# Twelve layers in one planned graph: the last block laid into the same plan and the same memory as the layers before it

## The chip, the cores and the metric

The kernel runs on one core of one Trainium2 chip. Its time is the device time of one execution in microseconds (us), taken as the median of several runs. Everything is float32, but for some masks in bfloat16.

## The reference

A decoder of four layers with three sublayers each, on `x` of 4 x 256 x 128 (batch, tokens, width), every sublayer added to its input:

```python
x = x + L0_attn(layernorm(x))
x = x + L0_xattn(layernorm(x), ctx_768, ...)
x = x + L0_ffn(layernorm(x), ...)          # grouped attention and experts
...
x = x + L2_attn(layernorm(x), ...)
x = x + L2_xattn(ctx_768, layernorm(x), mask, ...)
x = x + L2_ffn(layernorm(x), ...)          # 4-bit quantised, gated
x = x + L3_attn(layernorm(x), ...)
x = x + L3_xattn(layernorm(x), ctx_768, ...)   # 16 heads of 64
x = x + L3_ffn(layernorm(x), ...)          # six layers of local attention and a gated unit
```

The last sublayer, `L3_ffn`, is as long as a small network of its own:

```python
for i in range(6):
    x = attn_layer(shift_tokens(x), Wqkv[i], q_scale[i], k_scale[i], Wo[i]) + x
    x = ffn_layer(shift_tokens(x), ln_g[i], ln_b[i], W1[i], b1[i], W2[i], b2[i]) + x
```

`attn_layer` has 16 heads of 64; queries and keys are divided by their norm, scaled and turned by a rotary table, and every window of 32 queries sees its own and the previous 32 keys. `ffn_layer` is a layernorm, a product to 2 x 341, a gelu on one half, a product of the halves and a product back to 128.

## The kernel before

The kernel is a planner with two plans. Class `Flow` takes operations one by one (`op`): each has an engine, a weight (the time that the planner believes it takes), a unit of work, and the buffers that it reads, writes or holds. `order` then plays the graph through: at each step the operation that can start first is issued, and between several that can start the one with the earliest due time. A due time follows from the unit's place in the sequence of TensorE work (`bases`, stretched by a pace) and a number of its own for each kind of operation (the third entry in the tables `NET` and `LOCAL`). Each kind of buffer has a fixed number of slots; `vacant` tells when a slot is free. The instructions are written in that order, and on each engine they run in it.

Class `Net` plans the eleven sublayers up to `L3_xattn`: the stages are generators that yield after each batch, and the string `ORDER` says in which order their batches follow. Its last stages are `ffn2`, `attn3` and `X3`, the last for `L3_xattn`. Every kind of buffer is a set of tiles in pools that are closed when `Net` ends.

Class `LocalBlock` plans the last sublayer with another `Flow`, in pools of its own that take the memory that `Net` has given up:

```python
    with ExitStack() as early:
        d = Decoder(early, tc, a, const)
        d.prepare()
        with ExitStack() as own:
            Net(own, d).run()
    if "F3" in STEPS:
        LocalBlock(ctx, d).run()
```

`LocalBlock.run` first writes, outside of any plan, its constants (`prepare`: the rotary tables by SP, the window mask and memsets on POOL, L1780 to L1817) and its input (`start`: a layernorm of each batch, two transposes at L1824, copies on ACT at L1826 into `y`, which holds two batches with features on partitions). Then come six layers of four units, one for each batch (`unit`), and after every second batch a gated unit for both (`glu`). The weights of a layer are loaded by `load`, issued on ACT (L1840). A unit's steps bear these names in the plan: `project` (query and key products, L1775 through the helper `mm`), `square` (ACT, L1919), `cosine` and `turned` (DVE, L1921 and L1911), `rotary` (POOL, L1925), `norms`, `guess` and `newton` (DVE: inverse norms), `scale` (POOL, L1963), `turn` (transposes, L1973) and their copies (L1980), `scores`, `most`, `less`, `exp`, `sums` and `share` (POOL, L2007), `turn_p` (L2048) and its copies (L2053), `values`, `weigh`, `weigh_out` (L2071) and `out`. `finish` turns `y` back, adds it to `x` and stores, again outside of the plan.

In `Net` all products go through L371 and all transposes through L374; copies out of PSUM are at L379. L735 to L753, L646 to L653 and so on are the softmax steps of its attentions.

Of the kernel before, what the change touches and what calls it, by code (L numbers as in the profile page):

```python
# [66 lines left out]
class Decoder:  # L67
# [5 lines left out]
    def small(self, n, tag):  # L73
        return self.sm.tile([P, n], F32, tag=tag, name=tag, bufs=4)

# [7 lines left out]

    def rsqrt(self, out, in_, n, scale, eps, op=ALU.add):

        self.nc.vector.tensor_scalar(out, in_, scale, eps, ALU.mult, op)
        self.nc.gpsimd.tensor_tensor(out, out, self.neghalf[:, :n], ALU.pow)

    def layernorm(self, src, out, eps=1e-5):

        nc, n = self.nc, src.shape[1]
        st = self.small(6 * 4, "ln_st").rearrange("p (t s) -> p t s", s=6)
        mv = self.small(2 * 4, "ln_mv").rearrange("p (t s) -> p t s", s=2)
        rstd = self.small(4, "ln_rs")
        for t in range(n):
            nc.vector.bn_stats(st[:, t, :], src[:, t, :])
            nc.vector.bn_aggr(mv[:, t, :], st[:, t, :])
        self.rsqrt(rstd[:, :n], mv[:, :n, 1], n, 1.0, eps)
        for t in range(n):
            nc.vector.tensor_scalar(  # L100
                out[:, t, :], src[:, t, :], mv[:, t, 0:1], rstd[:, t : t + 1], ALU.subtract, ALU.mult
            )
# [63 lines left out]
class Flow:  # L166
# [11 lines left out]

    LAG = {"PE": 0.22, "ACT": 0.1, "DVE": 0.1, "POOL": 0.12, "SP": 2.5}
# [7 lines left out]
    def __init__(self, kinds, pace, patience, slots, lags, tables, tiles, free=(), dense=(), port=()):  # L187
        self.kinds, self.pace, self.slots, self.lags, self.tables = kinds, pace, slots, lags, tables
        self.patience, self.tiles, self.dense, self.port = patience, tiles, dense, port
        self.free, self.ops, self.counts = free, [], dict.fromkeys(slots, 0)  # L190

    def op(self, name, unit, fn, reads=(), writes=(), holds=()):
        eng, weight, late = self.kinds[name]
        op = {
            "name": name, "eng": eng, "w": weight, "late": late, "unit": unit, "fn": fn,
            "lag": self.lags.get(name, self.LAG[eng]), "table": self.tables.get(name),
# [21 lines left out]
    def bases(self):  # L218
        work = {}
        for op in self.ops:  # L220
            work[op["unit"]] = work.get(op["unit"], 0.0) + op["w"] * (op["eng"] == "PE")
        at, out = 0.0, {}
        for unit in sorted(work):
            at += work[unit] * self.pace
            out[unit] = at
        return out

    def order(self):
# [12 lines left out]
        made = dict.fromkeys(self.slots, 0)  # L241
# [21 lines left out]
        while len(done) < len(self.ops):  # L263
# [4 lines left out]
            for e, ops in waiting.items():  # L268
# [4 lines left out]
                if times:  # L273
                    first = min(t for t, *_ in times)
                    late = lambda o: o["due"] + (
                        (self.patience if o["tiles"][0] != shape else 0.0)
# [33 lines left out]
    def vacant(self, kind):  # L310

        out = []
        for slot, b in enumerate(self.held[kind]):
            if b is None:
                out.append((0.0, slot))
            elif all("end" in o for o in b.users):
                out.append((max(o["end"] + o["lag"] for o in b.users), slot))
        return sorted(out)

    def issue(self):  # L320
        for op in self.order():
# [3 lines left out]
            op["fn"]()  # L325


class Net:
# [12 lines left out]
        "top": (16, 6), "tr": (2, 6), "ss": (16, 2), "qs": (48, 4), "row": (128, 3),  # L341
    }
    SLOTS = {"bank": 8, "pad0": 2, "pad8": 2, "vb": 2, "vs": 2} | {k: n for k, (_, n) in TILES.items()}

    def __init__(self, ctx, d):
# [3 lines left out]
        tables = {k: "e" for k in NET if k.endswith("_exp")}  # L349
        self.flow = Flow(NET, NET_PACE, NET_PATIENCE, self.SLOTS, {"fetch": 6.0}, tables, NET_TILES, ("bank",))  # L350
# [6 lines left out]
    def buf(self, kind):  # L357
        if kind == "bank":
            return Buffer(kind, lambda i: self.pb.tile([P, 512], F32, tag=f"bank{i}", name=f"bank{i}", bufs=1))
        n, _ = self.TILES[kind]  # L360
        return Buffer(kind, lambda i: self.sb.tile([P, n], F32, tag=f"{kind}{i}", name=f"{kind}{i}", bufs=1))
# [641 lines left out]
    def prepare(self):  # L1003
        nc = self.nc
        make = lambda n, name: self.sb.tile([P, n], F32, tag=name, name=name, bufs=1)
        self.pads, self.vss, self.vbs = {}, [], []
        for hole in self.HOLE:
            self.pads[hole] = []
            for i in range(self.SLOTS[f"pad{hole}"]):
                m = make(256, f"pad{hole}_{i}")  # L1010
                nc.gpsimd.memset(m, 0.0)
                self.pads[hole].append(m)
        for i in range(2):

            v = make(1040, f"vs{i}")
# [3 lines left out]
        for i in range(2):  # L1019
            v = make(576, f"vb{i}")  # L1020
# [656 lines left out]
    def write(self):  # L1677
        stages = {name: getattr(self, f"stage_{name}")() for name in STEPS if name != "F3"}
        for name in ORDER.split():
            if name in stages:  # L1680
                next(stages[name])

# [42 lines left out]
class LocalBlock:  # L1725
# [15 lines left out]
        "qk": (1024, 5), "sq": (1024, 2), "tmp": (1024, 2), "ss": (64, 2), "rs": (64, 2),  # L1741
        "qT": ((8, P), 2), "mx": (16, 2), "p": (1024, 2), "rz": (16, 2), "vn": (1024, 3),
        "v": (1024, 2), "pT": ((8, P), 2), "oT": ((8, S), 1), "g_sq": (512, 1), "g_xc": (512, 1),
        "g_var": (4, 1), "g_rstd": (4, 1), "uT": ((3, 512), 1), "tab": ((2, 2, 2, 64), 2), "b1": (6, 2),
        "w4": (1024, 7), "w1": (2 * FF3, 2), "w2": ((3, D), 2),
    }
    SLOTS = {"bank": 8, "kT": 2} | {k: n for k, (_, n) in TILES.items()}

    def __init__(self, ctx, d):
        self.d, self.tc, self.nc, self.a = d, d.tc, d.nc, d.a  # L1750
        pool = lambda name, **kw: ctx.enter_context(self.tc.tile_pool(name=name, bufs=1, **kw))
        self.c, self.sb = pool("l_const"), pool("l_work")
        self.pb = pool("l_pb", space=PSUM)
        d.sm = self.sb
        tables = {"exp": "e", "gelu": "g"}
# [867 lines left out]
```

## Time and profile before

| | us |
|---|---|
| median of 3 runs | 2145.88 (2144.1 to 2146.22) |
| the profiled execution's own time | 2146.45 |
| span of the profiled execution | 2144.7 |
| TensorE busy in the span | 2040.7 (95%) |
| VectorE busy | 1635.6 (76%) |
| ScalarE busy | 1181.0 (55%) |
| GpSimd busy | 986.2 (46%) |

PE is TensorE, PEld its weight loads, DVE VectorE, ACT ScalarE, POOL GpSimd, SP the engine that issues most transfers. A row of the profile names line, engine, operation, the tiles written and read, and how often. "PEclk" is the clock that the throttle grants to TensorE, as a share of full speed; a busy TensorE at half clock does half the work. A float32 product appears as two records of TensorE. In a table of stretches each row is a part of the span with the busy time of each engine in it; in the chain of waits each piece is followed back to what released it.

### The profile page before, as it was taken

The numbers are of one execution on the slowest core, as the hardware profiler recorded it, in microseconds if no ns is written. First come the engines' busy times: TensorE is split into PE (matmuls) and PEld (weight loads), VectorE is DVE, ScalarE is ACT, GpSimd is POOL, SyncE is SP. The second block draws the span as 40 slices with busy tenths as digits, with TensorE's granted clock in tenths as the row PEclk, the third lists the DMA queues.
The fourth block names the chain that finished last, engine by engine and source line by source line (L and its number), as shares of the span: only waits on it lengthen the run. The fifth ranks groups of instructions, "written<-read, shape, count | busy, mean of one in ns | idle before, by whom it ended". The sixth has DMA issues, their size and how long they took to land.

```text
span 2144.7 us, 58806 instructions
## 1 busy us (share of the span) xinstructions
PE 2040.7 (95%) x24181; PEld 1347.1 (63%) x24181; DVE 1635.6 (76%) x4353; ACT 1181.0 (55%) x2668; POOL 986.2 (46%) x1152
## 2 busy tenths in 40 slices
PE   7999999999999998899999977999999999999997
PEld 4566585776665566566666644666666666666665
DVE  3766777788777758989986548978789787897882
ACT  1754736434536676566556534556555555565553
POOL 2333424331312234445333357756557565575660
PEclk6999999999999999899999988999999999999998
DMA  5000020002020000100000031112121121121101
GB/s 153 1 1 1 1 65 6 31 31 64 2 75 1 9 2 5 45 1 1 1 1 1 1 102 31 42 34 69 42 71 44 42 69 42 38 65 42 37 26 31
DMA packets 33419, 71.14 MB, mean 33 GB/s; under 512 B 5688, under 2 KB 17984, under 8 KB 33152
## 3 DMA queue, kind: packets, MB, share of 16 engines
q1 hardware_dynamic: 20320, 50.29, 8.1%
q10 hardware_dynamic: 12832, 17.09, 2.5%
q8 instruction: 191, 3.13, 0.6%
q14 instruction: 76, 0.62, 0.1%
HBM read 41.68 MB, written 0.52 MB: 20 GB/s over the span
## 4 chain that ended last, share of the span: by engine, by line
PE 70%; DVE 19%; POOL 5%; issue 3%; ACT 2%; DMA 1%; POOLq 0%; SPq 0%; DVEq 0%; ACTq 0%
PE bank L371 40%; PE bank L1775 18%; PE bank L374 8%; PE bank L1973 2%; DVE tmp L1911 2%; DVE ss L1926 2%; POOL qk L1963 2%; DVE qk L1921 2%; POOL qk L1925 1%; POOL p L2007 1%; PE bank L2048 1%; ACT sq L1919 1%; DVE p L735 1%; DVE rq L1947 1%; DVE rs L1948 1%
## 5 line engine op out<-in xcount | busy, mean ns | idle before, releaser
L1775 PE MATMUL bank<-w,ly 128*128 128x512 f32 x576 | 281.5, 611 | 0.4
L1925 POOL TENSOR_TENSOR qk<-qk,tmp 128x1024 f32<-128x1024 f32 x96 | 226.5, 2363 | 115.3 <-DVE tmp L1911 61.1
L653 POOL TENSOR_SCALAR p<-p,sums 128x508 f32<-128x508 f32 (+1 forms) x256 | 176.2, 696 | 215.7 <-DVE sums L650 203.7
L1963 POOL TENSOR_TENSOR qk<-qk,rs 128x1024 f32<-128x1024 f32 x96 | 181.0, 1904 | 78.3 <-DVE rs L1948 78.3
L648 ACT ACTIVATE p<-bank,nmx 128x508 f32<-128x508 f32 (+1 forms) x256 | 174.4, 690 | 76.0 <-DVE nmx L646 41.0
L371 PE MATMUL bank<-kx,qx 64*128 64x512 f32 (+3 forms) x1280 | 203.5, 523 | 1.6 <-DVE qx L629 0.9
L1919 ACT ACTIVATE sq<-bank 128x512 f32<-128x512 f32 x192 | 114.6, 600 | 137.5 <-PE bank L1775 113.0
L646 DVE TENSOR_REDUCE nmx<-bank 128x1 f32<-128x508 f32 (+1 forms) x256 | 165.0, 677 | 21.6 <-PE bank L371 21.2
L374 PE MATMUL bank<-ident,p 128*128 128x128 f32 x1312 | 174.2, 277 | 5.7 <-POOL p L749 3.8
L374 PEld LDWEIGHTS bank<-ident,p 128*128 128x128 f32 x1312 | 146.8, 141 | 50.4 <-issue 16.8
L950 ACT ACTIVATE pT<-bank 128x512 f32<-128x512 f32 (+1 forms) x256 | 124.9, 583 | 68.2 <-PE bank L371 67.3
L1921 DVE TENSOR_TENSOR qk<-bank,tab 128x512 f32<-128x512 f32 x192 | 127.8, 683 | 41.6 <-ACT sq L1919 35.3
L1775 PEld LDWEIGHTS bank<-w,ly 128*128 128x128 f32 x576 | 101.3, 194 | 82.6 <-issue 58.5
L371 PE MATMUL bank<-pT,big 128*64 128x256 f32 (+1 forms) x1280 | 149.5, 376 | 1.6 <-ACT pT L379 1.6
L2007 POOL TENSOR_TENSOR p<-p,rz 128x1024 f32<-128x1024 f32 x48 | 91.4, 1904 | 111.3 <-ACT kT L1980 62.6
L1911 DVE TENSOR_TENSOR tmp<-bank,tab 128x256 f32<-128x256 f32 x384 | 137.8, 410 | 1.6 <-ACT sq L1919 1.5
L927 DVE TENSOR_REDUCE pad<-bank 128x1 f32<-128x512 f32 (+2 forms) x256 | 116.7, 514 | 23.7 <-PE bank L371 23.4
L371 PEld LDWEIGHTS bank<-pT,big 128*64 128x64 f32 x1280 | 86.2, 137 | 69.1 <-issue 12.4
L379 ACT COPY pT<-bank 128x512 f32<-128x512 f32 (+2 forms) x208 | 102.4, 542 | 47.0 <-PE bank L374 45.5
L371 PEld LDWEIGHTS bank<-kx,qx 32*128 32x128 f32 (+1 forms) x1280 | 80.3, 184 | 67.8 <-issue 42.1
L1973 PE MATMUL bank<-ident,qk 128*128 128x128 f32 x768 | 102.2, 279 | 19.9 <-POOL qk L1963 19.7
L1973 PEld LDWEIGHTS bank<-ident,qk 128*128 128x128 f32 x768 | 87.5, 143 | 51.3 <-POOL qk L1963 31.2
(360 smaller groups left out, 4693.5 us busy)
## 6 DMA issues: line engine op xcount, KB each, us to landing
v<-vn SPq DMA_DIRECT2D x48, 384.0 KB, 3.9
x<-in_f_w SPq DMA_DIRECT2D x24, 512.0 KB, 3.7
w<-in_f_wqkv ACTq DMA_DIRECT2D x18, 512.0 KB, 7.9
v<-vn SPq DMA_DIRECT2D x48, 128.0 KB, 2.4
w<-in_f_wo ACTq DMA_DIRECT2D x6, 512.0 KB, 4.0
w<-in_f_w ACTq DMA_DIRECT2D x6, 341.0 KB, 3.9
w<-in_f_w ACTq DMA_DIRECT2D x6, 192.0 KB, 6.4
w<-in_x_wq SPq DMA_DIRECT2D x2, 512.0 KB
```

The lines of the kernel that those rows point to most:

```text
L371: self.nc.tensor.matmul(out, lhsT, rhs, start=start, stop=stop)
L374: self.nc.tensor.transpose(out, in_, self.d.ident)
L646: self.op("p_max", lambda ps=ps, one=one: nc.vector.tensor_reduce(one(nmx), ps.t[:, :n], AX.X, ALU.max, negate=True), [ps], [most], [nmx])
L648: self.op("p_exp", lambda ps=ps, one=one, cols=cols: nc.scalar.activation(cols(), ps.t[:, :n], AF.Exp, bias=one(nmx), accum_out=one(sums)) ...
L653: nc.gpsimd.tensor_scalar(cols(), cols(), one(sums), 1.0, ALU.mult, ALU.mult)
L1775: self.nc.tensor.matmul(out, lhsT, rhs, start=start, stop=stop)
L1911: nc.vector.tensor_mul(heads(tmp.t[:, cut])[:, :, lo : lo + 32], heads(ps.t)[:, :, 32 - lo : 64 - lo], spread(1, lo, lo + 32),)
L1919: op("square", lambda cut=cut, ps=ps: nc.scalar.activation(sq.t[:, cut], ps.t, AF.Square), [ps], [sq])
L1921: op("cosine", lambda cut=cut, ps=ps: nc.vector.tensor_mul(heads(out.t[:, cut]), heads(ps.t), spread(0, 0, 64)), [ps, w["tab"]], [out])
L1925: op("rotary", lambda: nc.gpsimd.tensor_add(out.t, out.t, tmp.t), [out, tmp], [out])
L1963: nc.gpsimd.tensor_mul(heads(out.t), heads(out.t), rs.t[:, at : at + 16, None].to_broadcast([P, 16, 64]))
L1973: nc.tensor.transpose(ps.t[:, i * P : (i + 1) * P], out.t[:, (g + i) * P : (g + i + 1) * P], d.ident)
```

## The change

The last block is written into the same `Flow` as the other layers. `Flow` takes several tables, each with its own pace and patience, and each operation carries those of its table. `ORDER` has four new entries `in`, one for each batch: `stage_in` makes the block's input from a batch of `x` as operations of the plan (at the first, also the constants: `room`, `constants`, `mask` in four pieces, `centred`). The block's units get numbers behind those of `Net`, so that their due times come later; `finish` is made of operations too (`align`, `end_turn`, `end_add`, `store`).

For memory, all buffers of `Net` and of the block lie in one tile, `arena`. Both have a `LAYOUT`, a list of kinds in order, from address 0; `Net` first lists what it gives up early, and the block what it needs first. For each slot of the block `after` lists the slots of `Net` that lie in the same place, and `vacant` gives it out only when all buffers of these kinds have been made and the last users of those slots have been planned. The 8 banks of PSUM are shared.

Smaller things: the keys `kT` have no padding of 32 columns before them any more, the first window reads columns 0 to 63 and has a mask of its own; the block uses the bfloat16 identity `ident16` of the other layers; the scratch tile `rq` is a buffer of the plan. All due times in `NET` and `LOCAL`, and the paces, are new; weights are the same. The core of the diff:

```diff
+    def __init__(self, parts, slots, lags, tables, tiles, free, dense, port, after):
+        self.kinds = {name: (*kind, *part[1:]) for part in parts for name, kind in part[0].items()}
...
             if b is None:
-                out.append((0.0, slot))
+                gone = [self.gone(*x) for x in self.after.get((kind, slot), ())]
+                if None not in gone:
+                    out.append((max(gone, default=0.0), slot))
...
+    def gone(self, kind, slot):
+        b = self.held[kind][slot]
+        if self.made[kind] < self.counts[kind] or b is not None and not all("end" in o for o in b.users):
+            return None
+        return max(o["end"] + o["lag"] for o in b.users) if b is not None else 0.0
...
+    LAYOUT = """
+    vb img ism im rtmp xin top tr h2T gates row pad8 pad0 q2 vs rz av ss imx oTs h qs ws x4 e2 o
+    w4 xT kx qx nmx sums p pT big st mv rs xn
+    """
...
+        self.at, size = _layout(self.LAYOUT, self.TILES)
+        at, most = _layout(LocalBlock.LAYOUT, LocalBlock.TILES)
+        after = {
+            slot: [k for k, (lo, n) in self.at.items() if lo < first + m and first < lo + n]
+            for slot, (first, m) in at.items()
+        }
+        self.at |= at
+        self.arena = self.sb.tile([P, max(size, most)], F32, tag="arena", name="arena", bufs=1)
...
+        self.last = LocalBlock(self)
+        stages["in"] = self.last.stage_in()
         for name in ORDER.split():
             if name in stages:
                 next(stages[name])
+        self.last.write()
...
+    LAYOUT = """
+    mask centre mean rot gains y l_w4:0-4 tab b1 w1 w2 l_ss l_rs rq qk sq l_w4:4-7 tmp
+    vn v qT kT mx l_rz l_p l_pT oT g_sq g_xc g_var g_rstd uT
+    """
...
+    def stage_in(self):
+        net, nc = self.net, self.nc
         for b in range(B):
+            net.n += 1
+            if b == 0:
+                self.prepare()
+            xn = net.buf("xn")
+            net.layernorm(net.tokens(b), [net.x[b]], net.tiled(xn), [xn])
+            ps = net.turned(net.tiled(xn), [xn])
+
+            def keep(b=b, ps=ps):
+                for h, y in enumerate(self.halves(b)):
+                    nc.scalar.copy(y, ps.t[64 * h : 64 * (h + 1), :S])
+
+            net.op("in_out", keep, [ps, self.y[b // 2]], [self.ys[b]])
+            yield
...
-                            r, at, to = slice(64 * e, 64 * (e + 1)), 32 * (4 * t + c), (c + 2 * e) % 4
+                            r, at, to = slice(64 * e, 64 * (e + 1)), max(32 * (4 * t + c - 1), 0), (c + 2 * e) % 4
...
 ORDER = """
 attn0 X0 attn0 X0 attn0 F0 X0 F0 attn0 F0 X0 A1 F0 F0 A1 X1 F0 F0 A1 X1 F0 ffn1 A1 X1 ffn1 A2 X1 A2
-ffn1 xattn2 A2 ffn1 xattn2 ffn2 A2 xattn2 attn3 ffn2 X3 xattn2 attn3 ffn2 X3 attn3 ffn2 X3 attn3 X3
+ffn1 xattn2 A2 ffn1 xattn2 ffn2 A2 xattn2 attn3 ffn2 X3 xattn2 attn3 ffn2 X3 attn3 ffn2 X3 in attn3 in X3 in in
 """
```

## The prediction

> **What bounds the kernel now.** I read the page first (busy shares and the row of granted clock), then stretches of the span one by one, then the chain of waits and finer stretches where the stretches are thin. The page says that TensorE is the engine to look at, and where its clock drops: in the first slice, around slices 16 and 17, and in slices 24 and 25.
>
> ```profile
> PE 2040.7 (95%) x24181; PEld 1347.1 (63%) x24181; DVE 1635.6 (76%) x4353; ACT 1181.0 (55%) x2668; POOL 986.2 (46%) x1152
> ...
> PEclk6999999999999999899999988999999999999998
> ```
>
> Cut into stretches (length, busy time of PE, PEld, DVE, ACT and POOL, then granted clock), the span is:
>
> ```profile
> core 0: us, PE busy (x) PEld busy (x) DVE busy (x) ACT busy (x) POOL busy (x), PEclk, DMA share, GB/s
> 60.00:810.00 750.00, 743.32 (x6348) 495.50 (x6346) 554.14 (x1770) 409.31 (x1043) 242.59 (x527) 1.00 0.07 21
> 810.00:890.00 80.00, 66.61 (x422) 46.05 (x421) 73.34 (x268) 50.70 (x163) 38.71 (x56) 0.89 0.07 19
> 890.00:1260.00 370.00, 364.37 (x2267) 230.06 (x2266) 291.27 (x819) 228.58 (x620) 149.01 (x207) 1.00 0.01 4
> 1261.50:1385.40 123.90, 96.00 (x1573) 63.45 (x1574) 100.32 (x230) 53.33 (x97) 89.93 (x67) 0.85 0.23 72
> 1385.40:2060.00 674.60, 654.42 (x12325) 437.62 (x12324) 556.31 (x1142) 392.39 (x661) 426.89 (x235) 1.00 0.17 48
> 2060.00:2144.70 84.70, 69.02 (x1120) 46.51 (x1118) 35.92 (x69) 36.42 (x62) 21.69 (x12) 0.93 0.12 33
> ```
>
> In 60 to 810, 890 to 1260 and 1385 to 2060 TensorE works 97 to 99% of the time at full clock: nothing is to be had there but by removing matmuls, and the change removes none. The thin places are 810 to 890, the join between the layers of Net and the last block (1261.5 to 1385.4), and the end. The change is made at the join. The chain through it:
>
> ```profile
> 1255.23 6.21 PE bank L371 x48
> ...
> 1264.15 1.13 POOL lmask L1795
> ...
> 1274.68 2.75 POOL ln_rs L87 x4
> ...
> 1277.97 0.75 PE bank L1824 x2
> ```
>
> Net's last matmul ends at 1261.4; then POOL builds the window mask (eight affine selects of 1.15 us and the memsets, 13.5 us of POOL in 14.3), and the reciprocal root of the layernorm, which is all that the first transposes wait for, stands behind it in POOL's queue. What follows is a pipeline filled from empty, at a clock that has dropped:
>
> ```profile
> 1275.80:1280.00 4.20, 4.07 (x17) 3.04 (x17) 2.17 (x7) 2.94 (x8) 3.56 (x9) 0.50 0.12 42
> ...
> 1306.40:1309.00 2.60, 2.52 (x9) 2.10 (x10) 0.43 (x1) 1.10 (x2) 2.60 (x3) 0.50 0.00 0
> ...
> 1324.00:1326.50 2.50, 0.28 (x1) 0.00 (x0) 2.50 (x4) 1.09 (x2) 2.50 (x2) 1.00 0.00 0
> 1326.50:1329.00 2.50, 2.42 (x28) 2.09 (x32) 2.26 (x10) 1.00 (x2) 0.03 (x1) 0.52 0.00 0
> 1329.00:1332.00 3.00, 3.00 (x120) 2.98 (x112) 2.90 (x9) 0.17 (x1) 2.08 (x2) 0.50 0.02 5
> 1332.00:1335.00 3.00, 3.00 (x14) 1.82 (x9) 2.68 (x5) 1.92 (x4) 3.00 (x2) 0.50 0.58 149
> ```
>
> ```profile
> PE bank L1824 <- issue: 14.5, 1, 14.5
> PE bank L1973 <- POOL qk L1963: 9.5, 2, 8.2
> PE bank L2048 <- POOL p L2007: 2.3, 1, 2.3
> ```
>
> These are TensorE's waits in the join: 14.5 us for the preparation, 8.2 until the first unit's queries are squared, normed and scaled, 2.3 until its probabilities are divided.
>
> **The join, priced.** TensorE is idle 123.9 - 96.0 = 27.9 us there. The steady stretch idles 3%, or 3.7 us in as long a time, so 24.2 us are the join's own. To this come the matmuls that ran slow: busy time by (1 - clock) over the fine stretches is 2.0 + 2.0 + 0.8 (1275.8 to 1288), 1.3 + 0.3 (1306.4 to 1312) and 1.2 + 1.5 + 1.5 + 0.9 (1326.5 to 1338), 11.5 us together. Sum 35.7. A count of the matmuls in the join (87 records of projections, 96 of turns, 512 of weighing, 768 of scores and so on, each at its cost in the layer from 1521.9 to 1659.4) comes to 87.2 us of steady time for 123.9, a loss of 36.7. I use 36: the most the join can give.
>
> **What the change moves there.** In the order in which the changed program's instructions stand on TensorE, Net's stages and the block are one sequence: the block's bias products and the first unit's eight query and key projections and four value projections stand among Net's last 150 matmuls. Behind the eighth projection there are still 24 transposes of Net (a row of twelve takes 2.84 us, so 5.5), 24 weighings (sixteen in 3.67, so 5.5), 16 output products (3.84) and five projections (0.86 each, 4.3): 19 us of work to cover the first unit's square, norm, root and scale, which took the 8.2 us of idle time before. The mask's and memsets' 13.5 us of POOL stand before the last ffn2 steps of Net; POOL is 40% busy between 890 and 1260, and who queues behind them there waits for one piece of some 3 us (two selects of 1.15 and the memsets). The layernorm's roots no longer queue behind them. So the 14.3 us, the 8.2 us and the slow clock after each are covered.
>
> **What stays.** From the first scores to the first turn of probabilities, most, less, exp, sums and share took 1314.4 to 1326.6, 12.2 us. In the new order there stand between them two small transposes (0.5), six projections (5.2), three turns of four (2.8) and the other scores (2.0), 10.5 us. About 2 us are open, as now. Here a rule is to be weighed. The row: 2.2 us without a matmul (1324.3 to 1326.5) is followed by a clock of 0.50 to 0.52 for some 9 us, at a cost of 5.1; another hole, of 2.9 us at 854.9, is followed by 0.52 as well. The Trainium skill, "TensorE: Matmul & The Clock Gate", section "Why this matters for your kernels", holds that the clock falls back when a gap is longer than about 3 us. By the rule the leftover hole costs only itself, 2.3; by the row 2.3 + 5.1 = 7.4, and the join would give 36 - 2.3 = 33.7 or 36 - 7.4 = 28.6. I go by the row, but at 6, since the hole comes out slightly shorter: 30.
>
> **The weights' loads.** ACT issued six loads in the join, while idle; the issues took 0.35, 1.55 for three, 0.58, and 4.28 for two[...]. In the new order they stand between ACT's exponents and copies of X3, where ACT is 62% busy; behind them wait exps and the copies of turned probabilities, and for those TensorE. Nothing to 6.5 us; in the block's layers the three take 2.43 and TensorE stays at 97%, so I take 1. SP's two table loads (rot, gains) move ahead of nothing that anyone awaits soon; their cover is the rest of X3, and if it went the cost would be the 3.6 us to landing.
>
> **Waits in the arena.** One tile for all buffers changes which waits are written: ACT's instructions wait on ACT itself 562 times for 256, on the rest as before. Most such waits are on work long done; ACT has 45% idle time and takes them before it waits for TensorE. Nothing to some 0.1 us each, an estimate from ACT's own rows, where an exp of 0.69 and its read of 0.19 follow each other without a hole that shows; I take 0. The keys' padding falls away with two memsets, the matmuls stay as many (14,099 in both programs): 0.
>
> **The new due times.** All due times are new, and Net's order on TensorE is the same as before in only about two thirds of its rows. 60 to 810 and 890 to 1260 have nothing to win. 810 to 890, where DVE is 92% busy, loses 13.4 us idle and about as much as 7 by the slow clock: 20 us could go. A second such place could arise as well. From +15 to -20; I take -2. In the block, 3% idle is 20 us over 675, mostly waits for POOL's scaling; -1, between +6 and -8. At the end (glu alone, 2114 to 2138) the chain is the same: 0.
>
> Sum: -36 + 6 + 1 - 2 - 1 = -32. The profiled execution took 2146.45 us (span 2144.7), the median of the runs is 2145.88: 0.6 apart, so I take the difference from the median: 2114.
>
> **Rivals.** (1) The fill moves but does not vanish. If X3's last exps, copies and DVE reductions are late because the block's squares and cosines (0.60, 0.68, 0.82 for two turns) are now between them, the first scale comes late and the 8.2 us hole with its cold clock (some 10 us) stays. Only the 14.3 us and the clock after it (4.8) go: about 19 less, less 1: 2128. For it: DVE is 88 to 96% busy in the fill. Against: 19 us of cover for 8. (2) The reorder also closes 810 to 890: 15 to 20 more, 2097. For it: it is the one thin place in Net. Against: DVE's work there is not reduced. (3) Slower: ACT's extra waits. 306 more waits on itself, each ahead of a copy or exp that TensorE waits for; if each put off the next matmul by more than 30/306 = 0.1 us, the join's gain would be gone, at 0.13 (40 us against a gain of 32) the time is 2154. Against: TensorE's idle time in the steady stretches is 1 to 3%, so most copies have slack. (4) The order is joined but the block's first reads wait for X3's end (its keys lie where p and pT lay): then only the preparation goes, as in (1); the interleaved rows speak against it.
>
> **How the numbers follow.** The join filled with one small hole, 2106 to 2122: 0.60, forecast 2114. Rivals (1) and (4), 2122 to 2135: 0.18. Rival (2), 2090 to 2106: 0.14. No change within 0.2% (4.3 us, about what a measurement of this kernel can tell): 0.03, a bad reorder eating the gain. Slower, (3) or a new thin stretch above 30 us: 0.05. The range takes in most of (1) and (2): 2097 to 2130.
>
> **What would show it.** Right: no stretch of 10 us near the end of X3 with TensorE under 7 us busy; the window mask on POOL before 1200; the granted clock 1.00 through the join but for one dip; the last block's first layer ending about 32 us sooner. Wrong: a POOL wait of 8 us before the first turns; a second stretch like 810 to 890; ACT issue or waits before the pT copies with TensorE waiting for them.

## The result, and the profile after

| | before | after |
|---|---|---|
| median, us | 2145.2 (4 runs) | 2126.64 (2121.23 to 2128.02, 4 runs) |
| ratio, with its 95% interval | | 0.9909 (0.989 to 0.9928) |
| the profiled execution's own time | 2146.45 | 2128.02 |
| its span | 2144.7 | 2126.2 |

The kernel is 18.6 us faster. The forecast was 32 less, 2114 us, and its range (2097 to 2130) held the time, near its upper end. The rest of this document is about the 13 us between the two.

The page of the changed kernel gives TensorE as busy 96% of the span, and this granted clock in 40 slices. Slices 24 and 25, the join, had an 8 each and have a 9 now; the dip in slice 17 is as it was.

```profile
PEclk6999999999999999899999999999999999999998
```

To see where the time came from, both spans are cut at the same instructions: at the gate product of `ffn2` on POOL (128x704; L1577 after) for two batches in succession, at the first `g_square` of the last block (ACT, L2097 before, L2136 after) and at its last one. I call the five pieces A to E. Stretches of the kernel before, columns as in the prediction; the rows are B, C, D and E:

```profile
core 0: us, PE busy (x) PEld busy (x) DVE busy (x) ACT busy (x) POOL busy (x), PEclk, DMA share, GB/s
...
1053.50:1122.40 68.90, 67.70 (x440) 43.53 (x437) 60.42 (x148) 42.78 (x114) 28.47 (x40) 1.00 0.00 1
1122.40:1385.40 263.00, 234.73 (x2421) 148.79 (x2420) 185.09 (x451) 135.96 (x309) 140.09 (x138) 0.93 0.11 35
1385.40:2122.40 737.00, 709.29 (x13402) 476.57 (x13400) 586.13 (x1199) 422.99 (x713) 447.57 (x246) 1.00 0.16 47
2122.40:2144.70 22.30, 14.15 (x42) 7.56 (x42) 6.11 (x11) 5.83 (x10) 1.01 (x1) 0.80 0.08 24
```

and of the changed kernel:

```profile
1051.40:1123.50 72.10, 71.35 (x443) 44.46 (x441) 62.48 (x148) 43.42 (x114) 46.71 (x58) 1.00 0.00 1
1123.50:1358.40 234.90, 223.21 (x2401) 142.41 (x2401) 185.60 (x443) 132.28 (x305) 127.78 (x122) 0.97 0.12 36
1358.40:2102.30 743.90, 713.61 (x13408) 478.81 (x13406) 588.06 (x1204) 423.50 (x715) 447.50 (x246) 0.99 0.17 47
2102.30:2126.20 23.90, 15.57 (x38) 7.58 (x38) 5.44 (x9) 6.01 (x10) 1.01 (x1) 0.68 0.04 11
```

Piece C, which holds the join, gave 28.1 us. Piece A gave 2.2. B, D and E took back 3.3 (from the unrounded marks), 6.9 and 1.6. Sum: -2.2 + 3.3 - 28.1 + 6.9 + 1.6 = -18.5, the difference of the two spans. So the join did what was forecast of it, and gain was given back in three other places.

**The join.** TensorE's waits in the changed kernel from Net's last matmul (1276.3) to the first `g_square`: the 14.5 us for the preparation and the 8.2 us for the first scaling are gone, the wait for the first probabilities has stayed and grown from 2.3 to 3.2 us.

```profile
PE bank L2086 <- POOL arena L2045: 4.7, 2, 3.2
PE bank L396 <- DVE arena L440: 1.2, 1, 1.2
PE bank L1796 <- ACT arena L2109: 1.0, 1, 1.0
```

The stretches around that hole show its second price, the clock:

```profile
1296.00:1300.00 4.00, 0.84 (x5) 0.77 (x5) 3.93 (x9) 1.09 (x2) 3.18 (x2) 0.84 0.00 0
1300.00:1304.00 4.00, 4.00 (x50) 3.98 (x48) 2.99 (x15) 1.17 (x2) 0.62 (x1) 0.50 0.00 0
1304.00:1308.00 4.00, 4.00 (x110) 3.42 (x107) 3.31 (x7) 1.07 (x2) 4.00 (x4) 0.50 0.07 16
1308.00:1312.00 4.00, 4.00 (x18) 2.48 (x18) 1.47 (x2) 3.12 (x6) 2.26 (x1) 0.88 0.44 119
```

Why 3.2 us and not the 2 that I had worked out: the order of POOL's queue. The timelines of POOL and of DVE at that place:

```profile
1292.65 4.68 POOL L1964 TENSOR_TENSOR arena<-arena 128x1024 f32<-128x1024 f32 x2 [4.84 <-DVE arena L1950]
1297.27 1.91 POOL L2045 TENSOR_TENSOR arena<-arena 128x1024 f32<-128x1024 f32 x1
```

```profile
1294.96 0.25 DVE L2042 RECIPROCAL arena<-arena 128x16 f32<-128x16 f32 x1
```

The reciprocal of the sums ends at 1295.2, the share (L2045) starts at 1297.27: it stands behind two rotary products (L1964, 4.68 us), though POOL had been idle for 4.84 us before them. A step that TensorE waits for queued behind steps of the next unit that nobody waited for yet. No run put the share in front of them.

**Piece B: VectorE slowed by the mask.** A hole that was not there before stands on TensorE's timeline of the changed kernel, ahead of transposes of `attn3`:

```profile
1128.10 0.66 PE L396 MATMUL bank<-ident,arena 128*128 128x128 f32 x2 [4.37 <-DVE arena L440]
```

It waits for VectorE, and VectorE is late because of what POOL does meanwhile. (The hole, 1123.7 to 1128.1, lies behind the mark that ends B, which is an instruction of POOL in the late chain. TensorE lost nothing in B itself; it got some 6 us of work further than without the mask, and paid at the start of C. In C the 6 us of work that were already done and the 6 us lost cancel.) VectorE's timeline in the quantising passes of `ffn2`, first before, then after, and below it POOL's at the same time (columns: start, duration of the whole group, engine, line, operation, tiles, how often):

```profile
1113.49 0.89 DVE L1541 TENSOR_TENSOR p<-p,qs 128x704 f32<-128x704 f32 x1
...
1115.51 1.82 DVE L1547 SCALAR_TENSOR_TENSOR x<-p,x 128x704 f32<-128x704 f32 x2
1117.36 0.53 DVE L1548 TENSOR_SCALAR x<-x 128x704 f32<-128x704 f32 x1
...
1118.55 3.66 DVE L1552 SCALAR_TENSOR_TENSOR x<-p,x 128x704 f32<-128x704 f32 x4
1122.13 0.18 DVE L1553 TENSOR_SCALAR qs<-qs 128x44 f32<-128x44 f32 x1
```

```profile
1109.41 1.40 DVE L1562 TENSOR_TENSOR arena<-arena 128x704 f32<-128x704 f32 x1
...
1112.29 1.82 DVE L1568 SCALAR_TENSOR_TENSOR arena<-arena 128x704 f32<-128x704 f32 x2
1114.14 1.35 DVE L1569 TENSOR_SCALAR arena<-arena 128x704 f32<-128x704 f32 x1
...
1115.53 5.66 DVE L1573 SCALAR_TENSOR_TENSOR arena<-arena 128x704 f32<-128x704 f32 x4
1121.11 1.13 DVE L1574 TENSOR_SCALAR arena<-arena 128x44 f32<-128x44 f32 x1
...
1123.59 1.65 DVE L1842 TENSOR_SCALAR arena<-ident 128x128 f32<-128x128 f32 x1
```

```profile
1104.25 2.34 POOL L1818 TENSOR_SCALAR_AFFINE_SELECT arena<-arena 32x1024 bf16<-32x1024 bf16 x2
...
1111.85 1.29 POOL L1815 MEMSET arena<- 32x1024 bf16 x1
1113.21 3.27 POOL L1818 TENSOR_SCALAR_AFFINE_SELECT arena<-arena 32x1024 bf16<-32x1024 bf16 x2
...
1118.84 3.35 POOL L1818 TENSOR_SCALAR_AFFINE_SELECT arena<-arena 32x1024 bf16<-32x1024 bf16 x2
```

The five rows here are longer by 0.51, 0.82, 2.00 and 0.95 us and, for L1568, not at all; with two smaller ones (L1560, 0.47 for 0.19; L532, 0.44 for 0.17) 4.8 us, and the centring at L1842 is 1.65 us of new work in the same queue: 6.5 us of delay on an engine that is busy 88% of B in the kernel before. (In e11 below, without the mask beside it, the centring stays where it is, takes 0.88 us, and there is no hole.) The selects suffer too (3.3 us for two, 2.34 undisturbed). Only the pair L1568, which began beside a memset, took its old 1.82. This is what the Trainium skill, "SBUF — State Buffer", section "Who interferes with whom", describes: an operation of VectorE with two operands in SBUF gets in the way of GpSimd's operations that read SBUF, not of those that only write it; VectorE's wide one-operand modes get in the way of both; and the one that comes second waits until the first is done. The trace agrees: of the four passes of L1573 the one that began beside a memset took 0.89 us, as before, and the three that began beside a select took 1.27 to 1.71; the memset at 1111.85, beside the one-operand pass L1566, took 1.29 us for 0.94. The hole of 4.4 us and 1.7 us of slow clock after it are as much as B is longer than with the same due times and no mask in it (see the first experiment: 66.3 without the mask, 72.1 with it).

**Piece D: the layers.** The longest waits of TensorE there, before (L1973 and L1963 are the turn and its scaling) and after (L2012 and L2002):

```profile
PE bank L1973 <- POOL qk L1963: 10.2, 15, 1.1
```

```profile
PE bank L2012 <- POOL arena L2002: 12.8, 15, 1.4
```

The new due times made this wait longer, up to 1.4 us in each layer. Five layers had such a hole; after the one in the third, the clock fell:

```profile
1682.00:1686.00 4.00, 2.60 (x83) 2.49 (x76) 3.97 (x9) 1.44 (x3) 3.48 (x2) 0.80 0.56 147
1686.00:1690.00 4.00, 4.00 (x15) 2.80 (x14) 0.03 (x1) 1.39 (x3) 4.00 (x3) 0.77 0.06 21
```

Of the 6.9 us, 2.6 are more idle time of TensorE (737.0 - 709.29 = 27.7, now 30.3) and 4.3 more busy time. Counted as busy time by (1 - clock) over stretches of 2 us, the slow clock makes 4.6 us in D, 1.5 before; 1.2 us of the busy time I cannot place. The idle time belongs to the due times: it is 30.1 to 30.6 us in the four joined kernels below that have the block's new ones (after, e7, e8, e11), and 25.4 to 28.3 in the six that have its old ones. For the slow clock in D the groups overlap: 4.9 to 8.0 us in the first, 1.7 to 8.0 in the second. Of the 6.9 us, then, some 2.6 are shown to be the due times'; how much of the slow clock they bring stays open.

**Piece E: the end.** The 1.6 us are not the due times': e7, e8 and e11 have the same ones, and an E of 22.5. In this execution the clock was at half for 10.2 us from 2104.2, in e7 for 6.8 us at the same place.

### The profile page after: what moved, and what is told of

It reads as the page before. It is cut to its first block, busy times and chain, and to the rows that moved or that the text cites. A ratio compares the mean times of both kernels' runs of the same rounds, so it can differ in the third digit from the quotient of the medians.

```text
span 2126.2 us, 59285 instructions
## 1 busy us (share of the span) xinstructions
PE 2036.1 (96%) x24181; PEld 1346.7 (63%) x24181; DVE 1638.7 (77%) x4352; ACT 1178.9 (55%) x2668; POOL 990.8 (47%) x1155
## 4 chain that ended last, share of the span: by engine, by line
PE 69%; DVE 21%; POOL 5%; issue 3%; ACT 2%; DMA 1%; POOLq 0%; SPq 0%; ACTq 0%; DVEq 0%
PE bank L393 39%; PE bank L1796 18%; PE bank L396 9%; PE bank L2012 2%; DVE arena L1950 2%; DVE arena L1960 2%; POOL arena L2002 2%; DVE arena L1965 2%; POOL arena L1964 1%; DVE arena L1573 1%; POOL arena L2045 1%; PE bank L2086 1%; DVE arena L2053 1%; DVE arena L2055 1%; DVE arena L1985 1%
## 5 line engine op out<-in xcount | busy, mean ns | idle before, releaser
L393 PE MATMUL bank<-arena 128*64 128x256 f32 (+11 forms) x6824 | 875.6, 395 | 11.5 <-ACT arena L1495 3.6
L393 PEld LDWEIGHTS bank<-arena 128*128 128x128 f32 (+4 forms) x6824 | 540.1, 166 | 291.1 <-issue 108.1
L1796 PE MATMUL bank<-arena 64*64 64x32 f32 (+3 forms) x13584 | 653.9, 251 | 11.4 <-ACT arena L2109 4.8
L1796 PEld LDWEIGHTS bank<-arena 64*64 64x64 f32 (+2 forms) x13584 | 387.9, 127 | 217.9 <-issue 119.8
L401 ACT COPY arena<-bank 128x512 f32<-128x512 f32 (+4 forms) x586 | 270.0, 489 | 295.2 <-PE bank L393 209.2
L396 PE MATMUL bank<-ident,arena 128*128 128x128 f32 x1757 | 257.1, 282 | 36.1 <-DVE arena L440 16.9
L396 PEld LDWEIGHTS bank<-ident,arena 128*128 128x128 f32 x1757 | 199.0, 143 | 134.3 <-issue 46.0
L1964 POOL TENSOR_TENSOR arena<-arena 128x1024 f32<-128x1024 f32 x96 | 226.5, 2363 | 123.1 <-DVE arena L1950 63.0
L675 POOL TENSOR_SCALAR arena<-arena 128x508 f32<-128x508 f32 (+1 forms) x256 | 175.8, 693 | 209.2 <-DVE arena L672 183.9
L670 ACT ACTIVATE arena<-bank,arena 128x508 f32<-128x508 f32 (+1 forms) x256 | 175.3, 691 | 79.1 <-DVE arena L668 36.6
L2002 POOL TENSOR_TENSOR arena<-arena 128x1024 f32<-128x1024 f32 x96 | 180.8, 1903 | 71.9 <-DVE arena L1986 71.9
L2045 POOL TENSOR_TENSOR arena<-arena 128x1024 f32<-128x1024 f32 x48 | 91.4, 1903 | 108.5 <-ACT arena L2018 62.7
```

The costliest lines, as they stand in the source:

```text
L393: self.nc.tensor.matmul(out, lhsT, rhs, start=start, stop=stop)
L396: self.nc.tensor.transpose(out, in_, self.d.ident)
L401: return self.op(name, lambda: copy(out(), in_()), reads, writes, holds)
L670: self.op("p_exp", lambda ps=ps, one=one, cols=cols: nc.scalar.activation(cols(), ps.t[:, :n], AF.Exp, bias=one(nmx), accum_out=one(sums)) ...
L675: nc.gpsimd.tensor_scalar(cols(), cols(), one(sums), 1.0, ALU.mult, ALU.mult)
L1796: self.nc.tensor.matmul(out, lhsT, rhs, start=start, stop=stop)
```

## The experiments

Every kernel is timed in five rounds against the kernel before on the same chip; the medians of before on the three chips lie between 2144.4 and 2146.6, so kernels of different chips are compared by their ratios. A to E are the five pieces of each profiled execution, in us; they say where a difference lies.

| kernel | median | ratio (95%) | A | B | C | D | E |
|---|---|---|---|---|---|---|---|
| before | 2144.4 to 2146.6 | 1 | 1053.5 | 68.8 | 263.0 | 737.0 | 22.3 |
| after | 2126.64 | 0.9909 (0.989 to 0.9928) | 1051.4 | 72.1 | 234.9 | 743.9 | 23.9 |
| e1_dues_only | 2145.59 | 1.0001 (0.999 to 1.0012) | 1051.3 | 66.3 | 265.3 | 739.7 | 21.9 |
| e2_old_dues | 2129.02 | 0.9915 (0.9899 to 0.993) | 1054.6 | 74.3 | 235.8 | 741.1 | 22.5 |
| e3_arena_only | 2146.23 | 1.0002 (0.9993 to 1.0011) | 1054.1 | 68.8 | 264.4 | 738.4 | 22.4 |
| e4_block_old_dues | 2122.61 | 0.9892 (0.9877 to 0.9907) | 1052.5 | 72.1 | 235.9 | 738.7 | 22.4 |
| e6_mask_in_net | 2134.81 | 0.9954 (0.9942 to 0.9967) | 1052.1 | 68.8 | 253.2 | 736.4 | 22.3 |
| e7_keep_warm | 2121.49 | 0.9894 (0.9881 to 0.9908) | 1046.7 | 72.1 | 233.7 | 743.8 | 22.5 |
| e8_mask_later | 2129.06 | 0.993 (0.9916 to 0.9943) | 1050.5 | 66.1 | 236.9 | 750.1 | 22.5 |
| e9_best | 2125.33 | 0.9909 (0.9888 to 0.9929) | 1052.2 | 66.1 | 237.1 | 742.9 | 22.5 |
| e10_block_warm | 2121.39 | 0.9879 (0.9861 to 0.9897) | 1046.6 | 72.2 | 233.3 | 740.7 | 22.5 |
| e11_mask_spread | 2126.08 | 0.9897 (0.9876 to 0.9918) | 1052.1 | 66.1 | 242.6 | 744.0 | 22.5 |
| e12_all_three | 2118.47 | 0.9866 (0.9848 to 0.9884) | 1052.4 | 66.1 | 238.2 | 739.0 | 22.3 |
| e13_mask_after_eight | 2121.19 | 0.9885 (0.9865 to 0.9904) | 1049.8 | 66.1 | 239.2 | 741.0 | 22.5 |

Piece A of e7, e10 and e13 is shorter for a reason that has nothing to do with their edits, told in the last section.

### The due times alone, and the joined plan without them

e1 is the kernel before with the new due times and paces; e2 the changed kernel with all the old ones; e4 has the new ones in Net and the old ones in the block. The edit, one row of the 224 for example:

```diff
 # e1, in NET of the kernel before
-    "p_share": ("POOL", 0.73, -186.5),
+    "p_share": ("POOL", 0.73, -146.34),
```

> The kernel before with the new due times, paces and patience in its two separate plans; graph, memory and constants as before. Theory A (the joined graph gives about 29 us, the new due times take back some 9: 2 in Net, 7 in the block's layers): 2150 to 2156 us, and the block's layer period, from one g_square to the next, near 138.0 where the old one is 137.4. Theory B (the due times are neutral, and the block loses by the shared arena's waits): 2145 within 3. Theory C (the new due times are better in themselves): under 2140.

> The changed kernel with the old due times, paces and patience for all kinds that it shares with the kernel before; the new kinds (constants, mask, room, in_out and so on) keep theirs. Theory A: the join's gain without what the new due times cost: 2114 to 2120. Theory B: 2127 within 4, since the arena stays. Theory C: the old due times don't fit the joined graph: above 2131.

> The changed kernel with the block's old due times and pace; Net's are the new ones. Theory A: the 7 us that the block's layers lost come back, 2118 to 2123, with no hole of 1.4 us at POOL's scale in each layer. Theory B: 2127 within 3.

The theory that e1 would be slower, at 2150 or more, fell: 1.0001. So did that of e2 at 2120 or less, where 2127 within 4 held; that of e4 held. In e1 piece A is 2.2 us shorter and D 2.7 longer: what Net gains the block's layers lose. (B is 2.5 shorter and C 2.3 longer, but that is the same work on the other side of the mark: TensorE's busy time is 2.2 less in B and 2.0 more in C.) e2, the joined plan by itself, gains 16.8 us (2145.83 to 2129.02, same chip). Against e2 Net's new due times take 4.9 us away by the ratios (e4: 0.9915 to 0.9892, with 4.2 us up to the first `g_square`), and the block's put 3.6 back (e4 to after: 0.9892 to 0.9909; 5.2 us in D of the profiles, of which 2.4 are idle time and 3.2 slow clock). In both steps the intervals overlap, so their sizes are rough; that the waits got longer with the new due times is not in doubt, since in e4 the longest is as before again:

```profile
PE bank L2012 <- POOL arena L2002: 9.9, 15, 0.9
```

### One tile for all buffers, nothing else

e3 is the kernel before, its order untouched, with the buffers of each of its two plans cut from one tile.

```diff
-        return Buffer(kind, lambda i: self.sb.tile([P, n], F32, tag=f"{kind}{i}", name=f"{kind}{i}", bufs=1))
+        return Buffer(kind, lambda i: self.arena[:, self.at[kind, i] : self.at[kind, i] + self.TILES[kind][0]])
```

> The kernel before with the same two plans and due times, but all buffers of a plan laid side by side in one tile, an arena for Net and one for the block; nothing else is moved and the order of instructions is the same. ACT then carries more waits on itself. Theory A: 2145 within 2. Theory B (each such wait costs on the path): 2150 or more, and the block's layer period longer by about a microsecond.

1.0002, with 0.9993 to 1.0011: the waits that a shared tile adds cost at most 0.1%, some 2 us. The slower rival is excluded.

### The mask alone moved into Net

e6 is the kernel before, but the window mask is built by operations of Net's plan during `X3`.

```diff
+        for w in range(4):
+            self.flow.op("l_mask", self.n, lambda w=w: build(w))
```

> The kernel before with two plans, but the window mask is built by POOL as four operations of Net's plan, in the middle of X3, and not at the join; the rest of the preparation (y, the keys' padding, tables, centre) stays at the join. Theory A: the mask is only part of what the join waits for; behind it stand the weights' issues on ACT (the last at 1268.5 in the profile of before) and their landing at about 1276, and the pipeline's fill. So 6 to 10 us less, 2136 to 2140. Rival (the join is the 11 us of mask and the clock that falls with it): 15 to 19 us less, 2127 to 2131. The fill's holes, 8.2 us before the first turns and 2.3 before the first turned probabilities, are there in either case.

2144.36 to 2134.81 on the same chip, 9.6 us; C is 9.8 us shorter. The theory had 6 to 10 in mind and the rival 15 to 19, so the first is right. TensorE's waits from Net's end to the first `g_square`:

```profile
PE bank L1982 <- POOL qk L1972: 10.5, 2, 9.4
PE bank L1833 <- issue: 4.2, 1, 4.2
```

The preparation's wait fell from 14.5 to 4.2, but the fill behind it stayed (9.4 us for the first scaling; 8.2 before). So of the joined plan's gain about a third is the mask, and the rest comes with the block's first unit put beside Net's last one. Here the mask cost nothing where it went: POOL was idle, VectorE had long pauses (9 of 15 us from 1185 to 1200 without work), the four selects below took 4.73 us, and TensorE has no hole before Net's end.

```profile
1192.07 4.73 POOL L1693 TENSOR_SCALAR_AFFINE_SELECT lmask<-lmask 32x1024 bf16<-32x1024 bf16 x4
```

### The residual hole kept warm

e7 is the changed kernel with three products ahead of the first `turn_p`, whose sums nobody reads.

```diff
+                    if (l, b, t, g) == (0, 0, 0, 0):
+                        for _ in range(WARM):
+                            self.mm(bank.t, d.ident, w["v"].t[:, :512])
```

> The changed kernel with three idle products of 128x512 (0.86 us each at full clock) in front of the first turn of probabilities in the block, into the bank that the turn then overwrites: TensorE works in the hole of 3.2 us in which it waits for POOL's share, and the turn comes as early as before. Theory A (the hole costs its length and about as much again by the half clock behind it): 4 to 5 us less than the changed kernel, 2120 to 2124, clock 1.00 behind the hole. Rival (the clock falls for another reason, such as the small products after the hole): no change, 2126 within 3.

The turns came as early as before and the time as expected, but not the clock: with the hole down to 0.6 us ahead of the turns it still fell to 0.50, for 6.8 us instead of 10.2. Why is open; behind the turns stand twelve products of one column (1.25 us), and the rival had small products in mind.

```profile
1296.00:1300.00 4.00, 4.00 (x138) 3.92 (x138) 3.76 (x16) 0.60 (x2) 2.41 (x2) 0.69 0.01 4
1300.00:1304.00 4.00, 4.00 (x8) 1.83 (x8) 2.93 (x5) 2.90 (x5) 4.00 (x3) 0.50 0.49 131
```

B and C together are 1.2 us shorter than in the changed kernel, the ratio says 3.2 (0.9909 to 0.9894, intervals overlapping); 4.7 us of its profile are piece A's and not the edit's. Worth 1 to 3 us, then, and not the 5 of the hole's slow clock.

### The mask at other places of the joined plan

e8 gives mask and centring to a unit three further on, so the planner orders everything behind it anew; e9 adds the block's old due times and the idle products to that. e11 keeps the plan's order and only issues the mask's sixteen instructions one at a time after later attention shares:

```diff
 # e8
-            flow.op("mask", n, lambda w=w: mask(w), writes=[self.mask])
+            flow.op("mask", n + 3, lambda w=w: mask(w), writes=[self.mask])
 # e11, in Flow.issue
+            if op["name"] == "mask":
+                pieces += op["fn"]()
+                continue
             op["fn"]()
+            if pieces and op["name"] == "p_share":
+                pieces.pop(0)()
```

> The changed kernel with the four mask operations and the centring given to a unit of work three further on, so that POOL builds the mask between the shares of X3, where DVE is some 60% busy, and not in the ffn2 stretch around 1105 to 1124, where DVE is the engine that sets the end. Theory A (POOL's mask slows DVE's quantising passes there, 1.3 to 1.7 us for passes of 0.9, and the layernorm behind them comes 4.4 us late for TensorE, with a slow clock after it): the hole at 1124 is gone, 5 to 7 us less, 2118 to 2122. Rival (the hole is one of the order, and POOL's product of the quantising queues behind the mask or not): the hole stays at 3 to 4 us, 2126 within 3.

> The changed kernel with three of the steps together: the block's old due times, the mask three units later, and the idle products in the first hole of the block. Theory A: the gains add, 4 + 6 + 4.5 below 2126.6: 2110 to 2115. Rival (they are the same time counted twice, since what is early at one place waits at the next): 2118 to 2122.

> The changed kernel with its plan and the order of every engine but GpSimd as they are; only the mask's 16 memsets and selects leave the place of 1103 to 1123 and come one at a time after the next 16 attention shares of X3 (from 1128 on). Theory A (the 4.4-us hole at 1124 and the slow clock after it, 6 us in all, come from GpSimd's selects beside VectorE's quantising passes of 128x704): hole gone, those passes at 0.9 us again, first g_square some 6 us earlier, 2119 to 2122. Rival (the selects are as much in the way of the shares, whose readers then wait, or the passes were slow for another reason): a hole of 2 us or more elsewhere before 1200, 2125 to 2129.

In both kernels B is 66.1 for 72.1 us, and VectorE's passes are as before; in e8:

```profile
L1573 DVE SCALAR_TENSOR_TENSOR arena<-arena 128x704 f32<-128x704 f32 x4 | 3.6, 892 | 0.1
```

So the 6 us of B are the mask's, shown twice. But neither kernel is measurably faster than the changed one (0.993 and 0.9897 for 0.9909): e8 and e9 are slower than either of their theories had it, and e11 is at its rival's number. In e8 the new order left a hole of 5.6 us before the first turns of probabilities (waiting for L2045) and 143.6 us from the first gated unit to that of the next layer (137.9 after); in e9 one of 5.6 us before other turns (L2012 for L2002), where the idle products do not stand. In e11 the pieces stood ahead of shares that TensorE's transposes wait for one by one:

```profile
PE bank L403 <- POOL arena L682: 3.9, 5, 1.3
```

3.9 us of waits and 1.6 of slow clock, nearly the 6 that B had won.

### Two and three edits together

e10 has the block's old due times and the idle products; e12 also the spread mask. e13 is e12 with the mask's pieces starting eight shares later.

```diff
 # e13 against e12, in Flow.issue
             if pieces and op["name"] == "p_share":
-                pieces.pop(0)()
+                seen += 1
+                if seen > 8:
+                    pieces.pop(0)()
```

> The block's due times and paces of before inside the joined plan, and three products of the identity with 512 columns, whose sums nobody reads, ahead of the block's first turns; the masks stay where the joined plan has them (1103 to 1129). Theory A (the terms add: the layers' 1.4-us holes cost 4 us, the clock after the hole at 1296 costs 5 us): 2116 to 2119, the clock 1.00 from 1300 to 1310. Rival (what is saved at the join is lost again in the layers, where a clock drop falls by chance): 2121 to 2124, as with either edit alone.

> Both of the other kernels' edits together: the block's due times and paces of before, the idle products ahead of its first turns, and the mask's pieces one at a time after the attention's shares. Theory A (all three terms add, 4 + 5 + 6 us off 2126.6): 2110 to 2114. Rival (they do not add, since a hole closed in one place opens in the next): 2118 to 2122.

> As the kernel with all three edits, except that the mask's sixteen pieces begin eight shares later (from about 1147 on), past the burst in which TensorE's transposes wait for every share. Theory A (a place for the mask where it neither slows VectorE's quantising passes nor stands ahead of a share that is waited for exists, and is worth the whole 5 to 6 us of idle time and slow clock between 1100 and 1150): the stretch 1100 to 1150 free of holes, as in the kernel before, first g_square some 5 us earlier than in the kernel with all three, ratio to before 0.983 to 0.985, 2108 to 2114. Rival (the pieces delay other shares, or the time is lost again before the end): a new hole after 1150 or none gained at the first g_square, ratio 0.986 to 0.988, 2115 to 2120.

e10 is at the rival's number by its median and, since its chip was slower for before too, between the two by its ratio (0.9879 of 2145.2, the median of before beside after, is 2119.2). The clock did not stay at 1.00 as theory A had it:

```profile
1297.00:1301.00 4.00, 4.00 (x122) 3.42 (x115) 3.79 (x15) 1.07 (x2) 2.55 (x2) 0.54 0.09 19
```

In e12 it did, behind a hole of the same length (1.05 us; 1.06 in e10) and the same products:

```profile
1300.00:1308.00 8.00, 6.76 (x154) 4.74 (x152) 7.66 (x25) 3.45 (x7) 4.21 (x3) 1.00 0.13 31
```

e12 is the fastest kernel here: 0.9866 (0.9848 to 0.9884), an interval wholly below that of the changed kernel (0.989 to 0.9928). At 2118.47 it is the rival's number, by the same conversion 2116.5 and between the two. The 15 us of theory A are not there, but the differences that e4, e7 and e11 showed one by one do add up: 3.6, 3.2 and 2.6 us by their ratios, 9.4 together, for 9.2 of e12. What was too large is the size expected of each. (All these intervals are as wide as the single gains.) D is 739.0, 2 us longer than in the kernel before, B has won its 6 us, and C carries the shares' waits (3.9) instead. In e13 the first 50 us behind the mask's old place are free of holes, but the pieces met the next burst of shares:

```profile
PE bank L405 <- POOL arena L684: 2.9, 5, 0.9
```

2.9 of waits and 1.6 of slow clock: the rival, and with a ratio of 0.9885 e13 is no faster than e12. Three places for the mask in the joined plan's order (1103, 1131 and 1140 onwards) cost 6, 5.5 and 4.5 us. The place that e6 suggests, some 12 us at once near 1188 where no share is in the queue, was not tried in the joined plan.

## Why the prediction was right, and where its size was off

The measured 2126.6 lies outside the 2106 to 2122 that I held most likely (0.60), and inside the 2122 to 2135 that I gave to rivals (1) and (4) with 0.18. What they describe did not happen. So the account of the join was right, but that the range held the time owes something to luck: it had been drawn wide for rivals that fell, and the cost that filled it is one that I had put at nothing. Point by point, by the prediction's own steps:

- **The join, -36, with +6 for the residual hole and +1 for the weights' issues: -29; measured -28.1 in C.** Right, and for the reasons given: work of Net and of the block stands behind the first unit's projections (19 us by my count) and covers its norm and scale; no wait of 8 us is left.
- **The residual hole.** It was forecast at somewhat under 2.3 us and was 3.2, since the share queued behind two rotary products; with 4.6 us of slow clock it cost 7.8, where 6 had been taken. At that length the Trainium skill's rule of about 3 us ("TensorE: Matmul & The Clock Gate", section "Why this matters for your kernels") leads to the slow clock as well as the row of before does, so this hole does not decide between them. Shorter ones do: 2.2 us before, and 1.4 us after with 0.77 behind it. But length is not all. Of five like holes of 1.4 us in D four cost no clock, and of the like holes of 1.05 us in e10, e12 and e13 two did and one did not. The same page's part on the HAM clock gate says that the clock is decided over a free-running window of some 3.4 us, so that the moment at which a hole falls matters; the traces agree: from a trace's first change of clock to its last, every stretch at half clock or at full lasts 3.41 us or a whole multiple of it.
- **The weights' issues, +1.** Too much. The first layer's stand at 1187 to 1198, where TensorE is busy 20.00 of 20 us (1180 to 1200). (The issues in the join of before that I listed are seven, not six.)
- **The mask at 0, because POOL was only 40% busy.** This step failed: +6. I priced who queues behind the mask on POOL, and not who works beside it. POOL was free, VectorE was not, and the two took turns. Busy time of the engine that does the work was the wrong thing to look at; 6 us (B, 72.1 for 66.1; a hole of 4.4 and 1.7 of slow clock on TensorE) is what it cost.
- **Arena waits, 0.** Right (e3, 1.0002).
- **Net's due times, -2.** Nearer -5 in the joined plan (e2 to e4), 2.1 of it in A and 2.2 in B. In two plans, and together with the block's, they were worth nothing (e1).
- **The block's due times, -1.** Wrong in sign, if inside its bounds (+6 to -8) but for a little: +6.9 in the profile of D, 5.2 of them gone in e4. Of these some 2.6 are the due times' for certain: the idle time that I hoped they would shorten, waits for POOL's scaling, became longer (12.8 us for 10.2). Most of the rest is slow clock, and these profiles do not show how much of it the due times bring.
- **The end, 0.** Right. The +1.6 of this profile, with a clock of 0.68 for 0.80 in the last 24 us, are gone in e7, e8 and e11, which end by the same plan.

Measured less forecast, in this one profile: mask +6, block +8, end +1.6, join +1, Net -3; together the 13 us between 32 and 18.6. The mask is the part with a cause shown by experiment; of the block's and the end's 9.6 us about a quarter is.

The rivals: (1) fell, the 8.2 us did not move along. (2) fell, the stretch around 810 to 890 lost as much as before and more (800 to 900: 13.6 us idle and 9.6 of slow clock, for 13.4 and 7.0). (3) fell with e3. (4) fell: 14.3 us of the block's products (L1796, 38 records) were done before Net's last matmul.

Of the signs that I had named, the mask before 1200 came true; the first layer was 27.0 us sooner and not 32. "No stretch of 10 us with TensorE under 7 us busy" failed narrowly at the residual hole (6.49 in 1290 to 1300) and, 150 us before X3's end, plainly at the mask's (5.63 in 1120 to 1130); with it came a second dip of the clock, at 1128.

## What to carry to other kernels

When work is moved into "idle" time of an engine, look at the engines that share something with it at that moment, not only at its own queue: twenty microseconds of GpSimd selects and memsets beside VectorE's full-width passes cost TensorE 6. A joined plan pays off where the first steps of the next phase can stand among the last ones of the one before (two thirds of this gain), and less by the mere removal of a preparation. And count every hole with its clock: one of 3.2 us cost 7.8, so a critical step queued behind a step that nobody waits for yet is worth an explicit place in the order, which no run here tried.

## What the runs showed of the hardware that was not expected

How long the start of the kernel runs at half clock differs from execution to execution, and the share in the profile's rows can hide it. From 20 to 60 us TensorE is busy throughout; in the changed kernel's profile, and then in e6's:

```profile
20.00:60.00 40.00, 39.40 (x111) 22.85 (x112) 17.02 (x49) 6.87 (x17) 6.48 (x18) 0.59 0.29 96
```

```profile
20.00:60.00 40.00, 38.92 (x112) 23.01 (x112) 16.96 (x50) 7.16 (x17) 6.44 (x18) 1.00 0.31 96
```

0.59 and 1.00, and yet as many matmuls in the same time. The same two records of a product of 96x512 in after, in e6 and in e7 show which figure to believe:

```profile
38.54 2.08 PE L393 MATMUL bank<-arena,ctxT 96*128 96x512 f32 x2
```

```profile
39.02 2.08 PE L372 MATMUL bank<-w,ctxT 96*128 96x512 f32 x2
```

```profile
36.77 1.13 PE L393 MATMUL bank<-arena,ctxT 96*128 96x512 f32 x2
```

2.08 us is the time at half clock, 1.13 the one at full. So TensorE ran at half clock in e6 too. The trace's list of clock changes begins only at 51.6 us there (51.2 in e13, which also shows 1.00), and a stretch without an entry counts as full clock. What did differ is when the clock rose for good: at 52.8 us in after, at 54.0 in e4, at 51.2 in e13, and at 48.3 in e7 and 48.0 in e10. Piece A ends later or earlier by about as much: e4 +1.1 us, e13 -1.6, e7 -4.7, e10 -4.8 against after. That is why an edit worth 3 us needs the pieces of a profile beside the ratio. It may also be one reason why the times of one kernel's runs lie 2 to 15 us apart; only one execution of each was profiled, so that is not shown.
